# A four-layer graph network on one Trainium2 core: in the fourth layer, full-array work and weighted values for two steps at once, the log of the adjacency added by VectorE, norms issued behind the ReLUs

## The chip, the cores and the metric

The kernel runs on one core of one Trainium2 chip. A core has a matrix engine (TensorE, PE in the profile, with its weight loads listed as PEld), a vector engine (VectorE, DVE), a scalar engine (ScalarE, ACT), a general engine (GpSimd, POOL) and a queue engine (SyncE, SP) that issues transfers. Matmuls write into banks of PSUM, which the kernel uses as tiles of 128 partitions by 512 float32; everything else works from SBUF. All arithmetic here is float32. The metric is the time of one execution in device microseconds; before the change it is 2323.35 us, the median of three runs (2322.41, 2323.35, 2325.75).

## The reference: what is computed

`x` has 128 graphs of 64 nodes with 256 features. Four pre-norm layers run one after the other, `x = x + layer(relu(layernorm(x)))`. The first three (a graph convolution with batch norms, a spectral one, an LSTM over skips) are not touched but for one helper stage. The fourth is graph attention over 512 edges (`src`, `dst`), 4 heads of 64 features:

```python
Xq = (H @ W_lin.T).reshape(bt, n, h, dh)
Xv = (H @ W_val.T).reshape(bt, n, h, dh)
e = einsum('behd,hd->beh', leaky_relu(Xq[:, src] + Xq[:, dst], 0.2), a)
e = e + log(A0[src, dst] + 1e-8)          # A0 is the adjacency
attn = softmax of e over the edges that share a src
Y = segment_sum(attn * Xv[:, dst], src)   # per graph and head
return Y @ W_out.T
```

## The kernel before

All rows are 128 × 64 = 8192, held in SBUF as 16 blocks `X[i]` of 512 rows (128 partitions × 4 × 256). Layer 3 (`layer3`, line 2439) runs 32 steps `g`; each is half a block, four graphs. Eight steps form a group `q` (32 graphs, 4 heads: 128 partitions), whose edge scores lie in one PSUM bank, `acc`. Five banks `ps` go round for everything else, and one pool of weighted values (`y2`) has the rest.

What one step does, by its functions:

- `turned` (line 2494): layer norm of a block, `h`, on ScalarE with factors `n_r`, `n_m` from VectorE; eight transposes on TensorE, `ps<-ident,h`; two copies into `hT`, by `move`, which gives every other copy to VectorE and the rest to ScalarE; then a few sums `hS`.
- `queries` (line 2524): seven products (Strassen's scheme) that give queries `Q` and values `XV` of a block. The last three products come in `rest`, and after them `linear` (line 2558): a product `lin_p` and two reductions on VectorE.
- `score` (line 2573), called S here: for each of eight (64-row) operands a matmul with the edge matrix, `ps<-ed_S,Q`, and a ReLU on ScalarE, `r<-ps`. Two neighbours use the upper and lower half of the array's rows and run at the same time. The matmuls are 64 rows × 128 columns.
- `reduce` (line 2586): eight matmuls `acc<-r,ed_apad` (128 rows × 64 columns) weigh the ReLUs with `a` into `acc`. For the first step of a group a matmul with one row, `acc<-ed_log,ones`, starts the bank with the log of the adjacency.
- ten steps later (`LAG = 10`, `v = g - 10`) the attention of step `v`: `spread` makes four products `aw` on VectorE, `gathered` adds them up by eight matmuls `ps<-aw,ed_ODT` (128 × 64) and a copy `an` on ScalarE; `weighted` (line 2721), called W here, makes `y<-an,XV`, 16 small matmuls 64 × 64; `output` (line 2737) multiplies with `W_out` (`ps<-w_o,y`), adds to `X` on VectorE and stores to memory.
- behind the last step of a group `summed` adds the linear part, `softmax` (line 2654) runs two scans, an exponential, two more scans, a reciprocal and a product on VectorE; `edgewise` transposes the result.
- in the first eight steps `back` (line 2281) still brings in the third layer's result: two copies into `ls_t` (one buffer), eight transposes and two adds to `X`.

The loop calls these step by step. At even `g` TensorE gets S, W, reduce, gather, then the transposes of the next block and one output; at odd `g`, S, W, reduce, gather, then queries, one output and the rest of the queries. `turn` (line 2599) runs the last steps, with the last softmax done by another way, in an order written out by hand (`nc.ordered`).

The order of the instructions on each engine is set when the kernel is built: a scheduler of the tile framework places them by its own model, unless `hold` or `ordered` adds a fixed order between two instructions of an engine. In the trace each engine's instructions follow that order. Pools with `bufs=n` give a new tile the storage of the one n before, and its first writer waits for the last reader of that one. A helper at line 799 records all operations, so every group in the profile has that line and is told by its tiles.

Of the kernel before, what the change touches and what calls it, by code (L numbers as in the profile page):

```python
# [1465 lines left out]
class Kernel:  # L1466
# [924 lines left out]
    def edges(self, w, pool, psum):  # L2391
# [33 lines left out]
        self.mm(p[0:1, :], self.ones[:N, 0:1], ga)  # L2425
        self.logA = w.tile([1, E], F32, name="ed_log")
        eps = pool.tile([1, 1], F32, name="ed_eps")
        nc.vector.memset(eps[:], 1e-8)
        self.act(self.logA[:], p[0:1, :], AF.Ln, bias=eps[:])
# [9 lines left out]
    def layer3(self):  # L2439
        nc, o, io = self.nc, self.o, self.io  # L2440
        cx, (w,) = self.stage([("l3x", 1)], "tile")
        with cx:
            cy, pools = self.stage([("l3", 2), ("l3v", 2), ("l3s", 1), ("l3r", 6), ("l3ps", 5), ("l3cps", 1), ("l3yps", 1)], "tile")
            with cy:
# [15 lines left out]
                self.queries(st, 0, WQV, *pools)()  # L2460
                for g in range(8 * NG):
                    v = g - LAG
                    ahead = (g + 1) // 2 if g % 2 and g + 1 < 8 * NG else None
                    self.score(st, g, *pools)
                    if v >= 1:
                        self.weighted(st, v - 1, *pools)
                    self.reduce(st, g, *pools)
                    if g % 8 == 1 and 1 < g:
                        self.edgewise(st, g // 8 - 1, *pools)
                    if v >= 0:  # L2470
                        self.between(st, v, *pools)
                    if g % 8 == 7 and g + 1 < 8 * NG:
                        self.summed(st, g // 8, *pools)
                    if g < 8:
                        self.back(8 + g, pools[4], "ps")
                    if ahead:
                        rest = self.queries(st, ahead, WQV, *pools)
                    elif g + 2 < 8 * NG:
                        self.turned(st, g // 2 + 1, *pools)
                    if g + 6 == 8 * NG:  # L2480

                        p = pools[4].tile([P, BT], F32, name="ps")
                        for c in range(4):
                            self.nc.tensor.transpose(p[:N, c * P:(c + 1) * P], self.OST[:, c, :], self.ident[:])
                        self.act_copy(self.cont[:N, :], p[:N, :])
                    if v >= 1 and g + 1 < 8 * NG:
                        self.output(st, v - 1, WO, *pools)
                    if ahead:
                        rest()
                    if g % 8 == 7 and g + 1 < 8 * NG:  # L2490
                        self.softmax(st, g // 8, *pools)
                self.turn(st, WO, pools)

    def turned(self, st, i, pool, vp, sp, rp, psum, psc, psy):

        h = self.norm(pool, i)
# [76 lines left out]
    def score(self, st, g, pool, vp, sp, rp, psum, psc, psy):  # L2573

        rs = st["r"] = []
        Q = st["Q", g // 2]
        for fc in range(2):
            for k in range(4):
                s = slice(64 * (k % 2), 64 * (k % 2) + 64)
                p = psum.tile([P, E], F32, name="ps")  # L2580
                self.mm(p[:], Q[s, 2 * (g % 2) + k // 2, fc * P:(fc + 1) * P], self.S2[s, :])
                r = rp.tile([P, E], F32, name="r", bufs=8)
                self.act(r[:], p[:], AF.Relu)
                rs.append(r)

    def reduce(self, st, g, pool, vp, sp, rp, psum, psc, psy):
# [3 lines left out]
        if i == 0:  # L2590
            st["acc", q] = psc.tile([P, E], F32, name="acc")
            self.mm(st["acc", q][:], self.ones[0:1, :], self.logA[:], True, False)
        for fc in range(2):
            for k in range(4):
                z = 64 - 32 * (k // 2) - 4 * i
                x = 64 * (k % 2)
                self.mm(st["acc", q][x:x + 64, :], self.apad[:, fc, z:z + 64], st["r"][4 * fc + k][:], False, False)

    def turn(self, st, WO, pools):
# [8 lines left out]
        self.output(st, v - 2, WO, *pools)  # L2608
# [6 lines left out]
        self.weighted(st, v - 1, *pools)  # L2615
# [21 lines left out]
        self.weighted(st, v, *pools)  # L2637

        late = lambda: None
        for v in range(8 * NG - 8, 8 * NG + 2):  # L2640
# [7 lines left out]
            if v <= 8 * NG:  # L2648
                self.weighted(st, v - 1, *pools)
# [20 lines left out]
    def shifted(self, st, q, pool, vp, sp, rp, psum, psc, psy):  # L2670
# [4 lines left out]
        scan(m[:], self.drop[:], acc[:], -FLOOR, op0=ALU.add, op1=ALU.max)  # L2675
        scan(m2[:, ::-1], self.dropr[:, ::-1], acc[:, ::-1], -FLOOR, op0=ALU.add, op1=ALU.max)
        o.tt(m[:], m[:], m2[:], ALU.max)
        o.sub(e[:], acc[:], m[:])
# [42 lines left out]
    def weighted(self, st, g, pool, vp, sp, rp, psum, psc, psy):  # L2721

        a, V = st["a", g], st["V", g // 2]

        yp = psy.tile([P, 2, E], F32, name="y2")
        for m in range(2):
            for h in range(HEADS):
                for x in range(2):
                    s, z = slice(64 * x, 64 * x + 64), slice(64 * (h % 2), 64 * (h % 2) + 64)
                    f = (2 * m + h // 2) * N  # L2730
                    self.mm(yp[z, x, f:f + N], V[s, 2 * (g % 2) + m, h * N:(h + 1) * N], a[s, m, h, :])
        y = st["y", g] = vp.tile([P, 2, 2, 2, N], F32, name="y", bufs=3)
        for x in range(2):
            (self.move if g < 8 * NG - 11 else self.act_copy)(y[:, :, :, x, :].rearrange("p f m s -> p m f s"),
                      yp[:, x, 0:4 * N].rearrange("p (m f s) -> p m f s", m=2, f=2))

    def output(self, st, g, WO, pool, vp, sp, rp, psum, psc, psy, late=False):

        y = st["y", g]
        out = self.io["out"].rearrange("b n d -> (b n) d")  # L2740
        parts = []
        for lo, hi in ((0, 1), (1, 2)) if g == 8 * NG - 1 else ((0, 2),):
            p = psum.tile([P, 2, D], F32, name="ps")[:, 0:hi - lo, :]
            for m in range(lo, hi):
                for f in range(2):
                    self.mm(p[:, m - lo, :], y[:, f, m].rearrange("p x s -> p (x s)"), WO[:, f, :], f == 0, f == 1)
# [68 lines left out]
```

## Time and profile before

| what | value |
|---|---|
| three runs | 2322.41, 2323.35, 2325.75 us |
| the profiled execution | 2319.09 us, span 2317.3 us, granted TensorE clock 0.998 |
| TensorE busy in the span | 2275.7 us (98%) |
| VectorE, ScalarE busy | 1622.4 us (70%), 1145.9 us (49%) |
| layer 3 in the profile | 1735.6 us to the end |
| its steps without attention | 1747.5 to 1848.6 us (TensorE busy 100.8) |
| its loop with attention | 1874.2 to 2243.0 us (TensorE busy 368.1, VectorE 245.5, ScalarE 147.2) |
| its tail, `turn` | 2243.0 to 2317.3 us |

The page's first part gives busy time and share of the span for each engine. The chain of work goes back from the last instruction, at each step to what released it. A timeline gives start, duration, engine, line, operation, output<-inputs, shapes and count of a group of neighbouring instructions, and in brackets the idle time before them and what ended it. A float32 matmul has two records, so a count of 16 is eight matmuls.

### The profile page before, as it was taken

Reading aid. Unit: us, or ns where it says so; the run is one execution under the profiler, and the core shown is the slowest. Engines: PE = TensorE matmul, PEld = TensorE weight load, DVE = VectorE, ACT = ScalarE, POOL = GpSimd, SP = SyncE. Lnnn points to the kernel's source line nnn. Section 1 sums busy time; section 2 is a strip of 40 time slices with the busy share of each in tenths; the row PEclk is TensorE's granted clock in tenths of the full one; section 3 lists DMA queues with packets and bytes.
Section 4 is the critical chain, followed back from the end, with each engine's and each line's share of the span. In section 5 each row is a group of like instructions: output and inputs, shape, how many; then the busy total and the mean of one; then the engine's idle time right before and its main releaser. Section 6 shows DMA issues by size and latency. Waiting matters only on the chain.

```text
span 2317.3 us, 32619 instructions
## 1 busy us (share of the span) xinstructions
PE 2275.7 (98%) x12113; PEld 1626.8 (70%) x12113; DVE 1622.4 (70%) x4040; ACT 1145.9 (49%) x2501; POOL 7.1 (0%) x33
## 2 busy tenths in 40 slices
PE   7999997999999999999999999999999999999999
PEld 4554445677777788888999998888885544554554
DVE  8887676887457777766767667559756676767667
ACT  5667765754445654443444444336435544444321
POOL 1000000000000000000000000000000000000000
PEclk9999999999999999999999999999999999999999
DMA  5000220230000000001000002000010000000001
GB/s 176 1 1 28 64 55 25 71 83 28 1 28 1 1 19 1 1 1 37 1 1 1 1 1 73 1 1 17 1 52 22 1 5 15 15 19 14 15 23 46
DMA packets 61066, 54.81 MB, mean 24 GB/s; under 512 B 15203, under 2 KB 58724, under 8 KB 60900
## 3 DMA queue, kind: packets, MB, share of 16 engines
q1 hardware_dynamic: 60900, 52.66, 7.4%
q8 instruction: 97, 1.59, 0.3%
q14 instruction: 69, 0.57, 0.1%
HBM read 35.86 MB, written 16.78 MB: 23 GB/s over the span
## 4 chain that ended last, share of the span: by engine, by line
PE 79%; DVE 3%; ACT 1%; issue 1%; ACTq 0%; DVEq 0%
PE ps L799 69%; PE acc L799 5%; PE pt L799 4%; PE y L799 1%; PE pe L799 1%; DVE aw L799 1%; DVE X L799 1%; DVE sm_m L799 0%; DVE XV L799 0%; ACT ls_g L799 0%; ACT h L799 0%; DVE ls_g L799 0%; ACT big L799 0%; DVE sm_e L799 0%; DVE lin L799 0%
## 5 line engine op out<-in xcount | busy, mean ns | idle before, releaser
L799 ACT ACTIVATE ls_g<-ls_g,ls_b 128x512 f32<-128x512 f32 (+4 forms) x472 | 243.1, 565 | 150.7 <-DVE ls_g L799 148.9
L799 ACT ACTIVATE ls_g<-ps,ls_b 128x256 f32<-128x256 f32 (+3 forms) x268 | 115.3, 470 | 329.5 <-PE ps L799 326.3
L799 PE MATMUL ps<-z,w 128*128 128x512 f32 x512 | 254.2, 618 | 0.0
L799 PE MATMUL ps<-big,X 128*128 128x176 f32 (+3 forms) x848 | 212.9, 367 | 0.1
L799 DVE TENSOR_TENSOR ls_g<-ls_z,ps 128x512 f32<-128x512 f32 (+5 forms) x256 | 147.0, 579 | 91.9 <-PE ps L799 90.3
L799 PE MATMUL ps<-ls_tx,X 128*128 128x160 f32 (+2 forms) x960 | 207.1, 327 | 1.4 <-DVE ls_tx L799 0.9
L799 DVE TENSOR_TENSOR aw<-at,ed_OST 128x1024 f32<-128x1024 f32 x128 | 150.0, 1219 | 83.0 <-PE ps L799 82.8
L799 PE MATMUL ps<-X,X 128*128 128x160 f32 (+1 forms) x896 | 199.1, 306 | 0.0
L799 PE MATMUL ps<-X,ls_w 128*128 128x256 f32 x640 | 190.5, 379 | 0.0
L799 PEld LDWEIGHTS ps<-ls_tx,X 128*128 128x128 f32 x960 | 161.8, 190 | 16.2 <-DVE X L799 4.7
L799 PEld LDWEIGHTS ps<-big,X 128*128 128x128 f32 x848 | 146.1, 190 | 29.6 <-issue 19.3
L799 DVE TENSOR_TENSOR X<-ls_g 128x1024 f32<-128x1024 f32 (+2 forms) x108 | 117.4, 1087 | 49.8 <-ACT ls_g L799 49.8
L799 ACT ACTIVATE r<-ps 128x512 f32<-128x512 f32 x256 | 131.6, 616 | 41.5 <-PE ps L799 41.5
L799 PEld LDWEIGHTS ps<-X,X 128*128 128x128 f32 x896 | 148.6, 190 | 0.0
L799 PE MATMUL ps<-X,ls_s 128*128 128x256 f32 x480 | 142.3, 379 | 0.0
L799 PE MATMUL ps<-ls_tx,ls_s 128*128 128x256 f32 x464 | 134.9, 379 | 0.0
L799 PE MATMUL ps<-ed_S,Q 64*128 64x512 f32 x512 | 132.9, 618 | 1.4 <-DVE hT L799 0.7
L799 PE MATMUL ps<-ls_tx,ls_w 128*128 128x256 f32 x464 | 133.4, 380 | 0.0
L799 PEld LDWEIGHTS ps<-X,ls_w 128*128 128x128 f32 x640 | 121.7, 190 | 16.5 <-DVE X L799 0.3
L799 PEld LDWEIGHTS ps<-z,w 128*128 128x128 f32 x512 | 86.7, 189 | 66.2 <-issue 58.6
L799 PE MATMUL ps<-big,ls_w 128*128 128x256 f32 x464 | 132.0, 380 | 0.7 <-ACT ls_z L799 0.7
L799 PE MATMUL ps<-aw,ed_ODT 128*64 128x512 f32 x512 | 117.3, 595 | 0.1
(550 smaller groups left out, 4012.1 us busy)
## 6 DMA issues: line engine op xcount, KB each, us to landing
X<-in_x_dram SPq DMA_DIRECT2D x32, 512.0 KB
xs<-X SPq DMA_DIRECT2D x16, 512.0 KB
X<-xs SPq DMA_DIRECT2D x16, 512.0 KB
out_dram<-X SPq DMA_DIRECT2D x31, 256.0 KB
X<-in_L_gnn_Wih_t_dram SPq DMA_DIRECT2D x4, 512.0 KB
ls_w<-in_L_gnn_Wih_t_dram SPq DMA_DIRECT2D x4, 512.0 KB
ls_w<-in_L_gnn_Whh_t_dram SPq DMA_DIRECT2D x4, 512.0 KB
w<-in_L_gnn_W_t_dram SPq DMA_DIRECT2D x2, 512.0 KB
```

Source lines behind the costliest of these rows:

```text
L799: i = method(*a, **kw)
```

## The change

- **Log of the adjacency.** It is kept on 128 partitions in place of one, and VectorE adds it to `acc` in `shifted`; the matmul that started the bank goes, and the first two matmuls of a group start it.
- **Two steps at once.** W of steps `v-2` and `v-1` are issued together at even `g`, into one `y` tile of two steps (two buffers in place of three of one step). All full-array work of a pair of steps is issued at the end of the odd one: queries, the output of step `v-3`, the rest of the queries, transposes of the next block, the output of step `v-2`. The first two blocks are transposed ahead of the loop. Two `back`s are issued at each odd `g` below 8 in place of one at every `g`. The softmax's transposes come in the odd step behind the first output; those of `ed_OST` at step 27 in place of 26.
- **Tail.** `turn` issues three outputs where it issued one, since the loop leaves two more to it.
- **Norms.** `normed`, new, makes the norm of block `g // 2 + 2` at even `g` with its ScalarE instructions held behind the ReLUs that `score` has just issued.
- **Scores.** Of each pair the operand in the lower rows (`x = 1`) is multiplied first; the ReLUs keep their order.

```diff
--- before.py
+++ after.py
@@ -2422,11 +2422,11 @@
         ga = cmp[:N, :]
         o.mul(ga, p[:N, :], self.OD[:N, :])
         p = psum.tile([P, E], F32, name="pe")
-        self.mm(p[0:1, :], self.ones[:N, 0:1], ga)
-        self.logA = w.tile([1, E], F32, name="ed_log")
-        eps = pool.tile([1, 1], F32, name="ed_eps")
+        self.mm(p[:], self.ones[:N, :], ga)
+        self.logA = w.tile([P, E], F32, name="ed_log")
+        eps = pool.tile([P, 1], F32, name="ed_eps")
         nc.vector.memset(eps[:], 1e-8)
-        self.act(self.logA[:], p[0:1, :], AF.Ln, bias=eps[:])
+        self.act(self.logA[:], p[:], AF.Ln, bias=eps[:])
 
         ac = self.columns(pool, "ed_ac", io["L3_gnn_a"].rearrange("h d -> (h d)"))
         self.apad = w.tile([P, 2, P], F32, name="ed_apad")
@@ -2458,42 +2458,49 @@
                 self.turned(st, 0, *pools)
                 WQV = self.sums3(w, WQV)
                 self.queries(st, 0, WQV, *pools)()
+                self.turned(st, 1, *pools)
                 for g in range(8 * NG):
-                    v = g - LAG
-                    ahead = (g + 1) // 2 if g % 2 and g + 1 < 8 * NG else None
+                    v, odd, last = g - LAG, g % 2, g + 1 == 8 * NG
                     self.score(st, g, *pools)
-                    if v >= 1:
-                        self.weighted(st, v - 1, *pools)
+                    if not odd and g + 4 < 8 * NG:
+                        self.normed(st, g // 2 + 2, pools[0])
+                    if last:
+                        self.weighted(st, [v - 1], *pools)
+                    elif v >= 2 and not odd:
+                        self.weighted(st, [v - 2, v - 1], *pools)
                     self.reduce(st, g, *pools)
-                    if g % 8 == 1 and 1 < g:
-                        self.edgewise(st, g // 8 - 1, *pools)
                     if v >= 0:
                         self.between(st, v, *pools)
-                    if g % 8 == 7 and g + 1 < 8 * NG:
+                    if not odd or last:
+                        continue
+                    if g % 8 == 7:
                         self.summed(st, g // 8, *pools)
                     if g < 8:
-                        self.back(8 + g, pools[4], "ps")
-                    if ahead:
-                        rest = self.queries(st, ahead, WQV, *pools)
-                    elif g + 2 < 8 * NG:
-                        self.turned(st, g // 2 + 1, *pools)
-                    if g + 6 == 8 * NG:
+                        for i in (7 + g, 8 + g):
+                            self.back(i, pools[4], "ps")
+                    rest = self.queries(st, (g + 1) // 2, WQV, *pools)
+                    if g == 8 * NG - 5:
 
                         p = pools[4].tile([P, BT], F32, name="ps")
                         for c in range(4):
                             self.nc.tensor.transpose(p[:N, c * P:(c + 1) * P], self.OST[:, c, :], self.ident[:])
                         self.act_copy(self.cont[:N, :], p[:N, :])
-                    if v >= 1 and g + 1 < 8 * NG:
-                        self.output(st, v - 1, WO, *pools)
-                    if ahead:
-                        rest()
-                    if g % 8 == 7 and g + 1 < 8 * NG:
+                    if v >= 3:
+                        self.output(st, v - 3, WO, *pools)
+                    if g % 8 == 1 and 1 < g:
+                        self.edgewise(st, g // 8 - 1, *pools)
+                    rest()
+                    if g + 3 < 8 * NG:
+                        self.turned(st, (g + 3) // 2, *pools)
+                    if v >= 2:
+                        self.output(st, v - 2, WO, *pools)
+                    if g % 8 == 7:
                         self.softmax(st, g // 8, *pools)
                 self.turn(st, WO, pools)
 
     def turned(self, st, i, pool, vp, sp, rp, psum, psc, psy):
 
-        h = self.norm(pool, i)
+        h = st.pop("h", None) or self.norm(pool, i)
         hT = st["hT"] = pool.tile([P, 2, BT], F32, name="hT", bufs=1)
         for dc in range(2):
             p = psum.tile([P, BT], F32, name="ps")
@@ -2575,13 +2582,21 @@
         rs = st["r"] = []
         Q = st["Q", g // 2]
         for fc in range(2):
-            for k in range(4):
-                s = slice(64 * (k % 2), 64 * (k % 2) + 64)
-                p = psum.tile([P, E], F32, name="ps")
-                self.mm(p[:], Q[s, 2 * (g % 2) + k // 2, fc * P:(fc + 1) * P], self.S2[s, :])
-                r = rp.tile([P, E], F32, name="r", bufs=8)
-                self.act(r[:], p[:], AF.Relu)
-                rs.append(r)
+            for k in (0, 2):
+                ps = [psum.tile([P, E], F32, name="ps") for x in range(2)]
+                for x in (1, 0):
+                    s = slice(64 * x, 64 * x + 64)
+                    self.mm(ps[x][:], Q[s, 2 * (g % 2) + k // 2, fc * P:(fc + 1) * P], self.S2[s, :])
+                for x in range(2):
+                    r = rp.tile([P, E], F32, name="r", bufs=8)
+                    self.act(r[:], ps[x][:], AF.Relu)
+                    rs.append(r)
+
+    def normed(self, st, i, pool):
+
+        self.nc.hold((None, None, self.nc.mark()[2]))
+        st["h"] = self.norm(pool, i)
+        self.nc.hold()
 
     def reduce(self, st, g, pool, vp, sp, rp, psum, psc, psy):
 
@@ -2589,12 +2604,12 @@
         q, i = g // 8, g % 8
         if i == 0:
             st["acc", q] = psc.tile([P, E], F32, name="acc")
-            self.mm(st["acc", q][:], self.ones[0:1, :], self.logA[:], True, False)
         for fc in range(2):
             for k in range(4):
                 z = 64 - 32 * (k // 2) - 4 * i
                 x = 64 * (k % 2)
-                self.mm(st["acc", q][x:x + 64, :], self.apad[:, fc, z:z + 64], st["r"][4 * fc + k][:], False, False)
+                self.mm(st["acc", q][x:x + 64, :], self.apad[:, fc, z:z + 64], st["r"][4 * fc + k][:],
+                        i == 0 and fc == 0 and k < 2, False)
 
     def turn(self, st, WO, pools):
 
@@ -2605,14 +2620,15 @@
         W = [self.spread(st, v, c, *pools) for c in (0, 2)]
         self.summed(st, q, *pools)
         e, m, m2 = self.shifted(st, q, *pools)
-        self.output(st, v - 2, WO, *pools)
+        for u in (v - 4, v - 3, v - 2):
+            self.output(st, u, WO, *pools)
         self.gathered(st, v, W, *pools)
         et = m2[:].rearrange("p (c b) -> p c b", c=4)
         p = psum.tile([P, 4, P], F32, name="ps")
         for c in range(4):
             nc.tensor.transpose(p[:, c, :], e[:, c * P:(c + 1) * P], self.ident[:])
         self.act_copy(et, p[:])
-        self.weighted(st, v - 1, *pools)
+        self.weighted(st, [v - 1], *pools)
         W = [self.spread(st, v + 1, 0, *pools)]
         p = psum.tile([P, P], F32, name="ps")
         for c in range(4):
...
@@ -2672,10 +2688,11 @@
         nc, o, acc = self.nc, self.o, st["acc", q]
         e, m, m2 = (vp.tile([P, E], F32, name="sm_" + x, bufs=1) for x in ("e", "m", "m2"))
         scan = nc.vector.tensor_tensor_scan
-        scan(m[:], self.drop[:], acc[:], -FLOOR, op0=ALU.add, op1=ALU.max)
-        scan(m2[:, ::-1], self.dropr[:, ::-1], acc[:, ::-1], -FLOOR, op0=ALU.add, op1=ALU.max)
+        o.add(e[:], acc[:], self.logA[:])
+        scan(m[:], self.drop[:], e[:], -FLOOR, op0=ALU.add, op1=ALU.max)
+        scan(m2[:, ::-1], self.dropr[:, ::-1], e[:, ::-1], -FLOOR, op0=ALU.add, op1=ALU.max)
         o.tt(m[:], m[:], m2[:], ALU.max)
-        o.sub(e[:], acc[:], m[:])
+        o.sub(e[:], e[:], m[:])
         self.act(e[:], e[:], AF.Exp)
         return e, m, m2
 
@@ -2718,32 +2735,32 @@
         a = st["a", g] = vp.tile([P, 2, HEADS, N], F32, name="an")
         self.act(a[:], A[:], AF.Copy)
 
-    def weighted(self, st, g, pool, vp, sp, rp, psum, psc, psy):
-
-        a, V = st["a", g], st["V", g // 2]
-
-        yp = psy.tile([P, 2, E], F32, name="y2")
-        for m in range(2):
-            for h in range(HEADS):
-                for x in range(2):
-                    s, z = slice(64 * x, 64 * x + 64), slice(64 * (h % 2), 64 * (h % 2) + 64)
-                    f = (2 * m + h // 2) * N
-                    self.mm(yp[z, x, f:f + N], V[s, 2 * (g % 2) + m, h * N:(h + 1) * N], a[s, m, h, :])
-        y = st["y", g] = vp.tile([P, 2, 2, 2, N], F32, name="y", bufs=3)
+    def weighted(self, st, gs, pool, vp, sp, rp, psum, psc, psy):
+
+        yp = psy.tile([P, 2, 2, 4, N], F32, name="y2")
+        y = vp.tile([P, 2, 4, 2, N], F32, name="y", bufs=2)
+        for k, g in enumerate(gs):
+            a, V = st["a", g], st["V", g // 2]
+            st["y", g] = y, 2 * k
+            for m in range(2):
+                for h in range(HEADS):
+                    for x in range(2):
+                        s, z = slice(64 * x, 64 * x + 64), slice(64 * (h % 2), 64 * (h % 2) + 64)
+                        self.mm(yp[z, x, h // 2, 2 * k + m, :], V[s, 2 * (g % 2) + m, h * N:(h + 1) * N], a[s, m, h, :])
+        n = 2 * len(gs)
         for x in range(2):
-            (self.move if g < 8 * NG - 11 else self.act_copy)(y[:, :, :, x, :].rearrange("p f m s -> p m f s"),
-                      yp[:, x, 0:4 * N].rearrange("p (m f s) -> p m f s", m=2, f=2))
+            (self.move if gs[-1] < 8 * NG - 11 else self.act_copy)(y[:, :, 0:n, x, :], yp[:, x, :, 0:n, :])
 
     def output(self, st, g, WO, pool, vp, sp, rp, psum, psc, psy, late=False):
 
-        y = st["y", g]
+        y, k = st["y", g]
         out = self.io["out"].rearrange("b n d -> (b n) d")
         parts = []
         for lo, hi in ((0, 1), (1, 2)) if g == 8 * NG - 1 else ((0, 2),):
             p = psum.tile([P, 2, D], F32, name="ps")[:, 0:hi - lo, :]
             for m in range(lo, hi):
                 for f in range(2):
-                    self.mm(p[:, m - lo, :], y[:, f, m].rearrange("p x s -> p (x s)"), WO[:, f, :], f == 0, f == 1)
+                    self.mm(p[:, m - lo, :], y[:, f, k + m].rearrange("p x s -> p (x s)"), WO[:, f, :], f == 0, f == 1)
             parts.append((p, lo, hi))
 
         def add():
```

More of the change, by code (lines that the diff above doesn't have):

```diff
@@ L2636, in turn @@
         W = [self.spread(st, v + 2, 0, *pools)]
-        self.weighted(st, v, *pools)
+        self.weighted(st, [v], *pools)
         late = lambda: None
@@ L2648, in turn @@
             if v <= 8 * NG:
-                self.weighted(st, v - 1, *pools)
+                self.weighted(st, [v - 1], *pools)
             late = self.output(st, v - 2, WO, *pools, late=True)
```

## The prediction

> **What bounds the kernel now.** First the page: busy shares, then the chain that ended last.
>
> ```profile
> PE 2275.7 (98%) x12113; PEld 1626.8 (70%) x12113; DVE 1622.4 (70%) x4040; ACT 1145.9 (49%) x2501; POOL 7.1 (0%) x33
> ...
> PE 79%; DVE 3%; ACT 1%; issue 1%; ACTq 0%; DVEq 0%
> ```
>
> TensorE (PE) is busy throughout. An edit pays if it takes time out of PE's own sequence, and costs if it makes PE wait. Then the windows of layer 3 (start of the layer, steps without attention, first attention step, the loop, the tail; columns PE, PEld, VectorE, ScalarE, POOL, granted clock, DMA share, GB/s):
>
> ```profile
> 1747.50:1848.60 101.10, 100.80 (x469) 54.24 (x468) 64.69 (x140) 56.68 (x107) 0.00 (x0) 1.00 0.00 1
> 1848.60:1874.20 25.60, 24.86 (x106) 12.13 (x105) 22.05 (x40) 13.52 (x26) 0.00 (x0) 1.00 0.00 0
> 1874.20:2243.00 368.80, 368.11 (x2271) 189.08 (x2270) 245.47 (x349) 147.21 (x290) 0.00 (x0) 1.00 0.05 15
> 2243.00:2317.30 74.30, 70.69 (x632) 37.50 (x630) 57.28 (x61) 14.71 (x35) 0.00 (x0) 1.00 0.13 43
> ```
>
> In the loop PE idles 0.7 us in 368.8, VectorE is two thirds busy, the clock is full and DMA near zero. So I price PE stretch by stretch, by starts of its instruction groups. An odd step, in PE's timeline:
>
> ```profile
> 2034.16 3.60 PE L799 MATMUL ps<-aw,ed_ODT 128*64 128x512 f32 x16
> 2037.69 1.13 PE L799 MATMUL ps<-w_qv,hT 128*128 128x256 f32 x4
> ...
> 2044.70 1.03 PE L799 MATMUL ps<-w_qv,hS 128*128 128x256 f32 x4
> 2045.66 3.91 PE L799 MATMUL ps<-ed_S,Q 64*128 64x512 f32 x16
> 2049.50 0.69 PE L799 MATMUL y<-an,XV 64*64 64x64 f32 x32
> ```
>
> From 2037.69 (T below) the queries with one output take 7.97 us, the next scores (S) 3.84, the weighted values (W) 0.62. VectorE beside it:
>
> ```profile
> 2045.69 1.23 DVE L799 TENSOR_TENSOR lin_p<-Q,ed_a 128x1024 f32<-128x1024 f32 x1
> 2046.84 0.68 DVE L799 TENSOR_TENSOR XV<-XV,ps 128x512 f32<-128x512 f32 x1
> 2047.43 2.43 DVE L799 TENSOR_REDUCE lin<-lin_p 64x16 f32<-64x1024 f32 x2
> ```
>
> These end at 2049.86, T+12.17, 4.2 us after the queries have left PE. Nobody on PE waits for the reductions now. Last, two spots where PE waits for VectorE or an engine is late:
>
> ```profile
> 1856.08 3.35 DVE L799 RECIPROCAL sm_m<-sm_m 128x512 f32<-128x512 f32 x1
> ```
> ```profile
> 1858.09 1.98 PE L799 MATMUL ps<-ed_S,Q 64*128 64x512 f32 x6
> 1860.81 2.84 PE L799 MATMUL ps<-ed_S,Q 64*128 64x512 f32 x10 [0.74 <-DVE hT L799]
> ```
> ```profile
> 1766.02 1.28 DVE L799 TENSOR_TENSOR X<-X,ps 128x512 f32<-128x512 f32 x2 [3.27 <-PE ps L799]
> 1767.22 0.64 DVE L799 COPY ls_t<-big 128x512 f32<-128x512 f32 x1
> ```
>
> The scores at 1860.81 stood until VectorE, held by the softmax's reciprocal, had copied hT out of a `ps` bank: five banks rotate, and a late copy holds scores that have nothing to do with it.
>
> **What the change saves on PE.**
>
> - Log of the adjacency: the `acc<-ed_log,ones` pair took 1.05 us from start to next start, four times; one lay in a start wait. 3 × 1.05 = 3.2. VectorE's add instead is one 0.68 us row per softmax, hidden, but for the tail (below).
> - Array shapes: PE pays when the matmul's shape changes. Steady passes of S are 0.423 us apart, the first after a change 0.527, the last before one 0.52; so a change costs 0.14 to 0.20 (to S 0.20, S to W 0.14, W to reduce 0.16, gather to full array 0.20, to transposes 0.16). A pair of steps had eight, 1.36 us; now W of both steps and the full-array work come once, six, 1.05. 10 pairs × 0.31 = 3.1, and 0.15 in each of five early pairs, 0.8. S and W that were split around other work (at 1975.7 and 2114.0, 0.66 each; at 1873.1, 0.95) and softmax transposes between narrow matmuls (2 × 0.3) are gone too: 2.9. Sum 6.8.
> - Norms behind the ReLUs: in steps 1, 3, 5, 7 ScalarE alternates `h` (0.49 a piece) with the ReLUs and S takes 4.89 in place of 3.84; in step 9 5.49, in step 11 4.87. 4 × 1.05 + 1.6 + 1.0 = 6.8.
> - Turned pairs: in S of 2026.15 a weight load waited 0.71 for a ReLU; with the bank that comes free later asked for first, both matmuls of a pair run side by side. Bounds for S: 0.527 + 6 × 0.423 + 0.52 = 3.58 and today's 3.84 to 3.90; I take 3.65, as ReLUs at 0.48 each still pace it, for the eleven odd steps that no other term touches: 11 × 0.22 = 2.4.
>
> Saved: 19.2 us. [...] Eight ReLUs at 0.48 take 3.9 us on ScalarE alone, more than S itself. [...]
>
> **What it costs.**
>
> - *Scores of even steps behind VectorE.* The odd step now runs queries, output, rest, transposes of the next block, output, and then S of the even step. The second half of hT is copied by VectorE, whose built order has it behind `lin_p` and both reductions. S would start at T + 7.97 + 0.87 (transposes) + 1.73 (output) = T+10.57, its second pair of matmuls at T+11.53, into the bank that the hT copy frees: T + 12.17 + 0.68 + 0.05 = T+12.9. The third pair needs the output's bank, added by VectorE next, at T+13.5. S becomes 5.1 in place of 3.84. Steps 14, 20, 22, 28: +1.22 each = 4.9. Steps 0, 2, 4, 6 (no outputs, but the same order; fourth pair late, S about 5.2): +1.35 each = 5.4. Behind the softmaxes (16, 24) two scans of 1.2 come ahead of the output's add: +2.0 each = 4.0. Steps 18 and 26 +0.75, 8 −0.15, 10 +0.55, 12 +1.05, 30 +0.25 by the same sum with their own fillings. Together 17.5. Ends: 0 if VectorE reaches the copy before T+11.5; 25 if each pair of every step also waits for its own add.
> - *Two `back`s in one step.* `ls_t` is one buffer. The second eight transposes need its refilling: by 1765.32 → 1767.86 VectorE ends it 2.54 after the first group's start, as two X adds (1.28) stand before it. Without the wait they would come after 0.93. With 0.1 to be released: +1.7, 4 times, 6.9. Ends: 3.2 (copy ahead of the adds, 1.75) and 8.3 (ScalarE's copy of 1.1 last).
> - *Norms ahead of the next ReLUs.* `normed` puts the square root and four `h` in ScalarE's order behind this step's ReLUs and so before the next step's. They wait for VectorE's factors. At step 9 the factors stand behind the softmax's 3.35 reciprocal: `h` would be done 27.3 after the full-array start of step 7, the first ReLU is due at 19.8: up to 7.5; lower end 3.35; I take 5.5, as VectorE's statistics may run earlier. Step 1 +0.8 (1.28 table load), step 11 +1.1, steps 17 and 25 +1.6 each (scans ahead). Together 10.6. Ends 0 and 14.
> - *Tail.* Two outputs move from the loop (−3.46) into `turn`, where VectorE is continuous from 2244 to 2250: three adds for one and the log add delay the softmax's later pieces by 3.5 to 3.75: +0.15. Start and the softmax of step 7: +1.3. Wider log (128 rows rather than 1): earlier stage, off the chain, 0.
>
> [...] At 1860.08 the hT copy ran only after the reciprocal and its product, and PE idled 0.74. [...]
>
> **Sum.** Costs 17.5 + 6.9 + 10.6 + 1.5 = 36.5, saved 19.2: +17.3. All durations are from the profiled execution (span 2317.3, 1.8 around it, 2319.1 in all), which lies 4.3 below the median of 2323.35; 2336.4 by its clock, 2340.6 against the median. I say 2340.
>
> DMA: `out` stores of two outputs a step go at once rather than one by one; SP's queue carries little (DMA share 0.05) and only the last store ends the span, where the tail is as before. POOL has nothing in the loop. Cost 0; without that cover a 256 KB store's landing would count, once.
>
> **Rivals.**
>
> 1. *The hT copy holds nobody* (other side). VectorE reaches the copy by T+11.5, or PE's order puts other work there. Then 17.5 goes: 2323, and with turned pairs at 3.65 in even steps perhaps 3 less, 2320: not slower. It decides where the copy ends: below 4.7 in all, a mean of 0.3 a step (copy done by T+11.9), the kernel is not slower by what can be told. For: the row at 1860.81 shows only 0.74 for a delay of 3.35. Against: T+12.17 for the reductions is measured, and the copy is behind them.
> 2. *VectorE becomes the bound.* The gathers wait for products `aw` (1.14 each). In a common pair the statistics end at about T+21.2 and the first product is released by T+22.1: 0.9 slack. If the waits push VectorE past it, each of ten pairs pays about 1: 2350. For: slack of 0.9 beside a 1.2 shift. Against: VectorE is idle 123 of 369 us in the loop, and PE's own waits give the slack back.
> 3. *No blocking by norms.* VectorE runs the factors early enough at steps 9, 17, 25: 10.6 goes: 2330. For: today's factors in common steps follow within 1 us of their inputs. Against: at 1862.37 they came after the reciprocal.
>
> That the change does not do what it says can hardly be: the removed matmuls have rows of their own.
>
> **How the numbers follow.** Mine 0.52 (range 2331 to 2350: ends of the three costs, taken half together); rival 1 0.22; rival 2 0.13; rival 3 0.13. A measurement here can tell 0.2%, 4.65 us, from no change. Faster (below 2318.7) takes half of rival 1 and a little of the ends, 0.13; same, the rest of rival 1 and part of rival 3, 0.15; slower 0.72. The range reaches from rival 1's lower part, 2319, to rival 2's middle, 2350, leaving out some 0.08 and 0.10.
>
> **What would show it.** Right: S of even steps 4.9 to 5.3 from start to next start with a weight load waiting for VectorE's hT; odd S 3.6 to 3.7; W as one group of 64 per pair; 2.5 between two `ls_t` groups; some 4 to 8 us of PE idle before S of step 9 with ScalarE on `h`; no `ed_log` rows on PE. Wrong: even S at or under 3.9 (rival 1); first gather passes waiting for `aw` (rival 2); S of step 9 as long as others (rival 3).

## The result and the profile after

The changed kernel takes 2347.52 us (median of five runs, 2345.04 to 2347.85) against 2323.35 us before: slower, ratio 1.0106, 95% interval 1.0095 to 1.0117. The forecast was 2340, from 2319 to 2350. The profiled execution took 2347.85 us, span 2346.1.

The first part of the page after, and the engines of its chain:

```profile
PE 2284.4 (97%) x12105; PEld 1633.6 (70%) x12105; DVE 1626.4 (69%) x4034; ACT 1148.1 (49%) x2490; POOL 7.2 (0%) x33
...
PE 75%; DVE 6%; ACT 1%; issue 1%; DMA 0%; DVEq 0%; ACTq 0%
```

VectorE's part of the chain doubled, from 3 to 6%, though its busy time is the same (1622.4 and 1626.4): it has become late at some places, not busier. The windows of the steps without attention, of the first attention steps and of the loop (columns as in the table before):

```profile
1753.90:1863.90 110.00, 100.91 (x467) 54.78 (x466) 65.27 (x139) 59.72 (x106) 0.00 (x0) 1.00 0.00 1
1863.90:1895.90 32.00, 26.87 (x108) 13.67 (x106) 19.95 (x38) 13.48 (x25) 0.00 (x0) 0.84 0.00 1
1895.90:2269.00 373.10, 366.55 (x2243) 188.91 (x2243) 253.73 (x383) 153.04 (x292) 0.00 (x0) 1.00 0.04 14
```

PE was idle for 0.3 us of the 101 before the softmaxes begin; now it is idle for 9.1 of 110. In the loop, 0.7 became 6.5.

**How the runs are compared.** Layer 3 starts between 1735.6 and 1742.6 us in the profiles below, though the layers ahead of it are the same but for one small matmul. So beside the times I give the length of layer 3: from its first transposes (`ps<-ident,h`, at 1735.62 before, at 1741.10 after) to the start of the last group of matmuls in PE's timeline, in one profile of each kernel. Before 574.5, after 597.7: 23.3 longer, near what the medians say (24.2).

Nearly all of that is in the scores, S: their start-to-next-start lengths add up to 132.0 us before and 154.9 after. The same sum over the even steps is 63.1 and 81.2, over the odd ones 68.9 and 73.7, where step 9 alone went from 5.49 to 11.68. The `ls_t` transposes went from 7.4 to 13.9, and the log's matmuls (4.2) are gone.

**An even S.** PE, its weight loads and VectorE around step 20 of the changed kernel, from their timelines:

```profile
2099.95 1.04 PE L799 MATMUL ps<-ident,h 128*128 128x128 f32 x8
2100.83 1.89 PE L799 MATMUL ps<-w_o,y 128*128 128x256 f32 x8
2102.65 1.98 PE L799 MATMUL ps<-ed_S,Q 64*128 64x512 f32 x6
2105.03 2.99 PE L799 MATMUL ps<-ed_S,Q 64*128 64x512 f32 x10 [0.40 <-DVE hT L799]
```
```profile
2105.03 0.30 PEld L799 LDWEIGHTS ps<-ed_S,Q 64*128 64x128 f32 x4 [1.23 <-DVE hT L799]
2105.75 0.44 PEld L799 LDWEIGHTS ps<-ed_S,Q 64*128 64x128 f32 x4 [0.42 <-DVE X L799]
2106.90 0.18 PEld L799 LDWEIGHTS ps<-ed_S,Q 64*128 64x128 f32 x1 [0.71 <-ACT r L799]
```
```profile
2101.82 2.43 DVE L799 TENSOR_REDUCE lin<-lin_p 64x16 f32<-64x1024 f32 x2
2104.29 0.69 DVE L799 COPY hT<-ps 128x512 f32<-128x512 f32 x1
2105.01 0.69 DVE L799 TENSOR_TENSOR X<-X,ps 128x512 f32<-128x512 f32 x1
```

The second matmul of the second pair stands until the hT copy ends at 2104.98, behind both reductions; the second of the third pair until the output's add at 2105.70; the last matmul then waits for a ReLU. S is 5.31. The weight loads of S in all, what they waited for, by the view of that tile (us, times), before and after:

```profile
  ACT r L799: 23.1, 45
  DVE XV L799: 3.0, 4
  DVE hT L799: 2.7, 3
...
  DVE X L799: 0.8, 3
```
```profile
  ACT r L799: 27.1, 56
  DVE hT L799: 21.8, 24
  DVE X L799: 9.3, 9
```

**Step 9.** VectorE, ScalarE and PE of the changed kernel from their timelines, and PE's windows (the last three figures are granted clock, DMA share and GB/s):

```profile
1872.04 3.35 DVE L799 RECIPROCAL sm_m<-sm_m 128x512 f32<-128x512 f32 x1
...
1876.64 0.16 DVE L799 SCALAR_TENSOR_TENSOR n_m<-n_mv,n_r 128x4 f32<-128x4 f32 x1
```
```profile
1876.83 2.07 ACT L799 ACTIVATE h<-X,n_m,n_r 128x256 f32<-128x256 f32 x4 [6.09 <-DVE n_m L799]
1878.81 2.02 ACT L799 ACTIVATE r<-ps 128x512 f32<-128x512 f32 x4
```
```profile
1871.47 2.84 PE L799 MATMUL ps<-ed_S,Q 64*128 64x512 f32 x10
1879.44 3.77 PE L799 MATMUL ps<-ed_S,Q 64*128 64x512 f32 x6 [5.13 <-ACT r L799]
1883.14 5.24 PE L799 MATMUL acc<-r,ed_apad 128*64 128x512 f32 x16
```
```profile
1874.30:1879.40 5.10, 0.01 (x1) 0.00 (x0) 4.25 (x16) 2.57 (x6) 0.00 (x0) 0.68 0.00 0
1879.40:1883.10 3.70, 3.66 (x6) 1.64 (x6) 0.00 (x0) 2.52 (x5) 0.00 (x0) 0.50 0.00 0
1883.10:1888.30 5.20, 5.20 (x17) 1.43 (x16) 0.00 (x0) 1.08 (x2) 0.00 (x0) 0.68 0.00 0
```

The norm's factors come behind the softmax's reciprocal, `h` behind them, the ReLUs behind `h`, and PE stands for 5.13 us. Its clock is then 0.50 through S and into the reduce, which takes 5.17 in place of 3.58.

**Two backs.** PE's timeline in an odd step below 8:

```profile
1771.26 1.09 PE L799 MATMUL ps<-ident,ls_t 128*128 128x128 f32 x8
1773.82 1.09 PE L799 MATMUL ps<-ident,ls_t 128*128 128x128 f32 x8 [1.46 <-DVE ls_t L799]
```

2.56 from one to the next, where 0.93 had been enough.

### The profile page after: what moved, and what is told of

Same layout as the page of the kernel before. It is cut to its first block, busy times and chain, and to the rows that moved or that the text cites. A ratio compares the mean times of both kernels' runs of the same rounds, so it can differ in the third digit from the quotient of the medians.

```text
span 2346.1 us, 32571 instructions
## 1 busy us (share of the span) xinstructions
PE 2284.4 (97%) x12105; PEld 1633.6 (70%) x12105; DVE 1626.4 (69%) x4034; ACT 1148.1 (49%) x2490; POOL 7.2 (0%) x33
## 4 chain that ended last, share of the span: by engine, by line
PE 75%; DVE 6%; ACT 1%; issue 1%; DMA 0%; DVEq 0%; ACTq 0%
PE ps L799 66%; PE acc L799 5%; PE pt L799 4%; DVE sm_m L799 1%; DVE lin L799 1%; DVE X L799 1%; PE pe L799 1%; PE y L799 1%; DVE lin_p L799 1%; DVE XV L799 1%; ACT h L799 0%; DVE aw L799 0%; DVE hT L799 0%; DVE Q L799 0%; ACT ls_g L799 0%
## 5 line engine op out<-in xcount | busy, mean ns | idle before, releaser
L799 PE MATMUL ps<-ed_S,Q 64*128 64x512 f32 x512 | 142.7, 629 | 14.5 <-DVE hT L799 5.9
L799 PEld LDWEIGHTS ps<-ed_S,Q 64*128 64x128 f32 x512 | 59.2, 187 | 87.9 <-issue 34.5
```

The costliest lines, as they stand in the source:

```text
L799: i = method(*a, **kw)
```

## The experiments

Twelve kernels, against the kernel before on the same chip. "Changed" is the kernel of the diff.

| kernel | median, us | ratio to before, 95% | layer 3, us |
|---|---|---|---|
| before | 2323.35 | | 574.5 |
| changed | 2347.52 | 1.0095 to 1.0117 | 597.7 |
| changed, linear part late | 2336.62 | 1.0043 to 1.0077 | 586.8 |
| changed, norms early | 2334.65 | 1.0036 to 1.0070 | 586.4 |
| changed, second back late | 2340.99 | 1.0064 to 1.0098 | 593.6 |
| changed, pairs not turned | 2339.32 | 1.0064 to 1.0097 | 591.7 |
| changed, one back a step | 2338.71 | 1.0057 to 1.0089 | 591.4 |
| changed, seven banks | 2324.25 | 0.9994 to 1.0012 | 574.8 |
| mended (four edits) | 2313.35 | 0.9948 to 0.9973 | 563.2 |
| mended, pairs turned | 2310.24 | 0.9938 to 0.9967 | 565.0 |
| mended, two ReLUs on VectorE | 2324.64 | 1.0002 to 1.0021 | 576.2 |
| mended, seven banks | 2301.53 | 0.9890 to 0.9923 | 552.5 |
| mended, seven banks, turned | 2302.69 | 0.9902 to 0.9933 | 552.6 |
| before, log on VectorE | 2324.05 | 1.0001 to 1.0019 | 577.1 |

My theory, A: even scores wait for VectorE's hT copy, norms hold the ReLUs behind a softmax, the second back waits for its buffer. The rivals are told with each run.

### The linear part behind the transposes

```diff
-            self.linear(st, i, pool, vp, sp, rp, psum, psc, psy)   # at the end of rest()
                     if v >= 2:
                         self.output(st, v - 2, WO, *pools)
+                    self.linear(st, (g + 1) // 2, *pools)
```

> The linear part (its product and two reductions on VectorE) is issued behind the next block's transposes and the second output, so that VectorE's order has the hT copy ahead of the reductions; nothing else moves. Theory A (even scores wait for the hT copy behind the reductions): in the changed kernel the sixteen even S hold 18.5 us above 3.92 each; with the copy ending at about T+10.5 rather than T+12.9 they come down to 3.9 to 4.2, and the time falls by 14 to 18 us, to about 2331. Rival (the even scores are slow for another cause, ScalarE's pace or the banks behind the output's add): S stays above 5 in steps 14, 20, 22, 28 and the time falls by less than 4. Second rival (the reductions only move the wait to the products aw): S is short, but the gathers wait, gain below 8.

Layer 3 is 11.0 us shorter. VectorE and PE in the steady loop of this kernel:

```profile
2060.05 0.68 DVE L799 COPY hT<-ps 128x512 f32<-128x512 f32 x1
2060.65 1.20 DVE L799 TENSOR_REDUCE lin<-lin_p 64x16 f32<-64x1024 f32 x1
```
```profile
2060.87 3.95 PE L799 MATMUL ps<-ed_S,Q 64*128 64x512 f32 x16
2064.76 1.16 PE L799 MATMUL y<-an,XV 64*64 64x64 f32 x64
```

S is in one piece, 3.88 in steps 14, 20, 22 and 28, 3.90 in steps 2, 4 and 6; the even steps' sum fell from 81.2 to 65.3, by 15.9. That is theory A's step, and the rival (another cause) is out. But 5.3 us came back in odd steps: S of step 17 went from 4.85 to 6.58, of step 25 from 4.84 to 8.03. The reductions now run later, with them the softmax, and its reciprocal and the norm behind it (ScalarE's `h` waits for the factors, and the ReLUs, from 2145.08, stand behind `h`):

```profile
2137.34 3.35 DVE L799 RECIPROCAL sm_m<-sm_m 128x512 f32<-128x512 f32 x1
```
```profile
2142.62 2.07 ACT L799 ACTIVATE h<-X,n_m,n_r 128x256 f32<-128x256 f32 x4 [0.68 <-DVE n_m L799]
```

Where the norms are made earlier as well (the mended kernels), both S are 3.90 to 3.92.

### The norms one step earlier

```diff
-                    if not odd and g + 4 < 8 * NG:
-                        self.normed(st, g // 2 + 2, pools[0])
+                    if (not odd and g % 8 or not g or g % 8 == 7) and g + 4 < 8 * NG:
+                        self.normed(st, (g + 1) // 2 + 2, pools[0])
```

> The norms that the changed kernel makes at steps 8, 16, 24, behind a softmax on VectorE, are made one step earlier, behind the ReLUs of steps 7, 15, 23 and ahead of the softmax. Theory A (norms waiting for factors behind the softmax hold the next ReLUs): S of step 9 falls from 11.68 to about 4, its reduce from 5.17 to 3.6, S of steps 17 and 25 from 4.85 to 3.92: 11 us less, about 2336. Rival (VectorE itself is late there with Q or hT, and the norms only share the wait): S of step 9 stays above 8 and the gain is under 4.

11.4 us shorter, as A had it. PE's timeline at step 9 of this kernel:

```profile
1871.48 3.98 PE L799 MATMUL ps<-ed_S,Q 64*128 64x512 f32 x16
1875.40 3.65 PE L799 MATMUL acc<-r,ed_apad 128*64 128x512 f32 x16
```

S of step 9 is 3.92, its reduce 3.58, S of steps 17 and 25 3.92.

### The two backs

```diff
                         if g < 8:
-                            for i in (7 + g, 8 + g):
-                                self.back(i, pools[4], "ps")
+                            self.back(7 + g, pools[4], "ps")
...
                     rest()
+                    if g < 8:
+                        self.back(8 + g, pools[4], "ps")
```

> The second back of steps 1, 3, 5, 7 is issued behind the rest of the queries in place of directly behind the first one. Theory A (its transposes wait for the one buffer ls_t to be filled again): the two groups of ls_t transposes of a step take 0.9 each and no longer 2.5 for the first, 6.5 us less in the four steps; some of it may come back as even S waiting longer for VectorE, which has two more adds ahead of the hT copy: total gain 3 to 6.5, about 2342. Rival (the banks, freed by adds to X, are what is late): the wait only moves, gain under 1.5.

The two groups of transposes take 7.2 us in all in place of 13.9, but layer 3 is only 4.1 shorter: the wait moved. In the changed kernel with this edit VectorE adds the second back ahead of its hT copy (VectorE, then PE):

```profile
1782.51 1.28 DVE L799 TENSOR_TENSOR X<-X,ps 128x512 f32<-128x512 f32 x2
1783.72 0.68 DVE L799 COPY hT<-ps 128x512 f32<-128x512 f32 x1
```

S of steps 2, 4, 6 and 8 went from 5.17, 5.17, 5.17 and 3.94 to 7.54, 7.49, 5.93 and 6.18: 7.7 longer in all, more than the 6.7 that the transposes won. Layer 3 is shorter all the same because of step 9, which the edit was not meant for. In ScalarE's new order three of its ReLUs stand ahead of `h`; its S is 3.92 in place of 11.68, and the wait for `h` comes in the reduce, which takes 8.57:

```profile
1876.98 1.93 PE L799 MATMUL acc<-r,ed_apad 128*64 128x512 f32 x6
1881.23 4.40 PE L799 MATMUL acc<-r,ed_apad 128*64 128x512 f32 x10 [2.31 <-ACT r L799]
```

That is 4.4 less for the two together. So I returned to one back a step, at the end of even steps too:

```diff
+                    if g < 8:
+                        self.back(8 + g, pools[4], "ps")
                     if not odd or last:
                         continue
-                    if g < 8:
-                        for i in (7 + g, 8 + g):
-                            self.back(i, pools[4], "ps")
```

> One back at every step below 8 as in the kernel before, ahead of the odd step's other full-array work; all else as changed. Theory A (two backs in a row wait for the one buffer ls_t): 64 ls_t transposes take 7 to 8 us in all and no longer 13.9, against one more change of the array's shape in even steps (0.15 each): 5 to 6 us less, about 2341. Rival (the work added ahead of the hT copy matters more than the buffer, as when the second back was put behind the queries): even S of steps 2 to 8 lengthen and the gain is under 2.

6.4 us shorter, S as in the changed kernel but for 0.3 more in steps 7 and 15. The buffer's wait was worth 6 us, and the work put ahead of the hT copy was dearer than the buffer in the first try.

### The pairs not turned

```diff
-                for x in (1, 0):
+                for x in (0, 1):
```

> The pairs of the scores are multiplied upper rows first, as in the kernel before; all else as changed. The prediction's own step (turned pairs make S 0.2 shorter): odd S goes from 3.92 to 4.1 or more, 2 to 4 us slower, 2350. Rival (ScalarE's ReLUs, eight at 0.48, pace S whichever half comes first): odd S stays 3.9 and the time within 1 us.

Neither: 6.1 us *shorter*. Odd S is 3.90 against 3.92, so turning brought nothing there; even S of steps 14, 20, 22 and 28 is 4.64 against 5.31. The even steps hold 3.4 of the 6.1; another 1.8 lies in step 9 (S 10.56 for 11.68, its reduce 4.53 for 5.17), where the clock was at 0.50 for 6.8 us and no longer 10.2, and 0.5 in step 1. The weight loads of such an S without turning:

```profile
2098.12 0.29 PEld L799 LDWEIGHTS ps<-ed_S,Q 64*128 64x128 f32 x2 [0.72 <-ACT r L799]
2098.64 0.29 PEld L799 LDWEIGHTS ps<-ed_S,Q 64*128 64x128 f32 x3 [0.22 <-DVE hT L799]
```

The trace does not name the banks, but the waits tell which engine each matmul waited for. In the turned S of step 20 above, the fourth waits for the hT copy and the sixth for the output's add. Here the fourth waits for the first ReLU, and the fifth for the hT copy. The late bank comes a place later: the fourth matmul starts 1.87 after S (at 2098.12), and the wait for hT holds the fifth until 2.39; turned, nothing but the third runs from 0.96 until the hT copy lets the fourth go at 2.38.

### All four edits

> All four undone or mended: linear part behind transposes and second output, norms of steps 8, 16, 24 one step earlier, one back a step, scores' pairs not turned; the log on VectorE, the weighted values of two steps and the full-array work of two steps stay. Theory A (the costs are these and the savings of the prediction are real: 3.2 log, 6.8 array shapes, 6.8 norms out of the ReLUs): even and odd S 3.9, time 2347.5 - 16 - 12 - 6 = about 2313, some 9 us under the kernel before. Rival (the savings are not real, the new order has its own price): 2322 or more.

2313.35 us, ratio 0.9960: faster than before. Layer 3 is 34.6 us shorter than changed; the four edits one by one gave 11.0, 11.4, 6.4 and 6.1, 34.8. That the two agree so closely is in part chance: the early norms also win back most of the 5.3 that the late linear part lost in odd steps, and beside these edits turning costs 1.8 and not 6.1 (next run). The costs lie in these four places, then, and what is left is a saving: 11.3 us under the kernel before. The prediction's savings without the turned pairs, less its 1.5 for tail and start, come to 15.3; S of step 0, for one, still takes 5.39 for 3.84. How much of the 11.3 is the log's was not tried by itself. A steady pair of steps takes 33.50 against 33.74 with S 0.06 longer: 0.30 for two changes of shape less, where the prediction had 0.31.

> As the one before, with the scores' pairs turned as in the changed kernel. Theory A after the first runs (turning costs because it asks first for the bank that VectorE frees late, and gains nothing as ScalarE paces S): with the hT copy early the two orders are within 1 us. The prediction's own step: turned is 2 to 5 us faster.

1.8 us longer in layer 3 than not turned (565.0 and 563.2), the times' intervals overlap. With the hT copy early the order of the pairs hardly matters.

### What paces S

S was 3.84 to 3.92 in every undisturbed step, not 3.65. Two of the ReLUs on VectorE:

```diff
-                    self.act(r[:], ps[x][:], AF.Relu)
+                    if 4 * fc + k + x in (3, 7):
+                        self.o.ts(r[:], ps[x][:], 0.0, ALU.max)
+                    else:
+                        self.act(r[:], ps[x][:], AF.Relu)
```

> As the mended kernel, with two of each step's eight ReLUs on VectorE (maximum with zero) in place of ScalarE. If ScalarE's 0.48 a ReLU paces S, odd S falls from 3.9 to about 3.6 where VectorE is free, up to 8 us in all, less what waits for VectorE in even steps. If the array paces S, odd S stays 3.9 and the time is the same or longer.

Odd S stayed 3.90, and layer 3 grew by 13.0 us, as the reduces (122.0 us in all against 112.5) and gathers (119.9 against 115.0) waited for VectorE. The test was badly chosen, though: when five banks go round, the third and fourth pair of S take the banks of ReLUs 0, 1 and 2, and I had moved 3 and 7. It doesn't tell ScalarE from the banks. This does:

```diff
-            ("l3ps", 5), ("l3cps", 1), ("l3yps", 1)
+            ("l3ps", 7), ("l3cps", 1)
...
-        yp = psy.tile([P, 2, 2, 4, N], F32, name="y2")
+        yp = [psum.tile([P, 2, 4, N], F32, name="ps") for x in range(2)]
```

> The mended kernel with the two PSUM banks that only the weighted values used put into the common pool: seven banks go round in place of five, and the weighted values take two of them per pair of steps. If S is paced by the way of the first ReLU back to the sixth matmul's bank (five banks), S falls from 3.9 to the unhindered 3.6 in nearly all 32 steps, 6 to 10 us less, about 2304. If the array or ScalarE's sum of eight ReLUs paces S, it stays at 3.9 and the time within 2 us. Beside it the transposes and outputs have more banks too: even S wait less for VectorE.

2301.53 us, ratio 0.9906, the best of all. PE's timeline in its loop:

```profile
2067.31 3.70 PE L799 MATMUL ps<-ed_S,Q 64*128 64x512 f32 x16
2070.95 1.16 PE L799 MATMUL ps<-an,XV 64*64 64x64 f32 x64
...
2079.06 3.70 PE L799 MATMUL ps<-ed_S,Q 64*128 64x512 f32 x16
```

S is 3.63 in thirty of 32 steps, even and odd, with the same eight ReLUs on ScalarE. So the wait for a bank that a ReLU gives back paced S: its weight loads waited 13.1 us for ReLUs in the mended kernel and 3.8 in this one. With pairs turned:

> Seven banks with the scores' pairs turned. If turning matters only where the second bank of a pair comes free later than the first, it makes no difference where no bank is waited for: within 1 us of the run before. If turning has a price or gain of its own in the array, S differs from it by 0.05 or more in every step, 2 us or more in all.

552.6 against 552.5, and S the same in 30 steps: with seven banks turning made no difference. Last, seven banks in the changed kernel alone:

> The changed kernel with one edit: the weighted values' two banks go into the common pool (seven banks in place of five); VectorE's order, the norms and the two backs stay as changed. If the even scores wait because a bank comes round too soon, not because of VectorE's order by itself, seven banks move the hT copy's bank from the second pair of S to the third: T+12.9 against 12.4, so even S falls from 5.3 to 4.1 to 4.3, odd S to 3.63, S of step 9 stays long (it waits for ReLUs behind the norms): 16 to 22 us less, about 2328. If the scores need the hT copy or VectorE in another way, even S stays above 5 and only the odd ones gain: 4 to 6 us.

2324.25 us: 23.0 us of layer 3 come back by one edit. Even S is 4.29 or 4.30 in steps 14, 20, 22 and 28, odd S 3.63 but for steps 1, 9, 11, 17 and 25, S of step 9 still 10.28:

```profile
1871.91 2.07 PE L799 MATMUL ps<-ed_S,Q 64*128 64x512 f32 x2 [4.58 <-ACT r L799]
```

So the even scores waited for banks that came round too soon, not for the hT copy itself, and step 9 is another thing, the order on ScalarE.

### The log alone

The four hunks on the log, put into the kernel before (log on 128 partitions, `o.add(e, acc, logA)` in `shifted`, no matmul at the group's start).

> The kernel before with one part of the change alone: the log of the adjacency on 128 partitions, added by VectorE in the softmax in place of the matmul that starts the bank. The prediction's own step: three of the four matmul pairs, 1.05 us each, lie on the path, VectorE's add is hidden but for the last softmax (0.7): 2.5 to 3.2 us less. Rival (the add delays a softmax that something waits for, at steps 9 and 17 and in the tail): no gain, within 1 us.

The rival: layer 3 is 2.6 us *longer*, ratio 1.0010 (1.0001 to 1.0019). The matmuls (4.2) are gone, but S grew by 5.1: steps 8, 16 and 24 by 0.8, 1.5 and 0.7, steps 9, 17 and 25 by 0.5, 0.4 and 1.2, and the tail loses half a microsecond. PE's and VectorE's timelines at step 9, where PE before had waited 0.74:

```profile
1862.18 2.84 PE L799 MATMUL ps<-ed_S,Q 64*128 64x512 f32 x10 [1.24 <-DVE hT L799]
```
```profile
1857.45 3.35 DVE L799 RECIPROCAL sm_m<-sm_m 128x512 f32<-128x512 f32 x1
1860.83 0.69 DVE L799 TENSOR_TENSOR sm_e<-sm_e,sm_m 128x512 f32<-128x512 f32 x1
1861.44 0.68 DVE L799 COPY hT<-ps 128x512 f32<-128x512 f32 x1
```

The matmul's time goes on PE, but the softmax, and the hT copy behind it, end later where VectorE was already late for PE. Only the sum was tried: whether the add alone or the scheduler's new order after it (step 8's S is split around other work there) has the larger part is open.

## Why the prediction was right, and where it was not

- **Even scores (17.5):** right. The copy was forecast to end at T+12.86 and the add at T+13.5; with T = 2092.08 (S's start less 10.57) that is 2104.94 and 2105.58, measured 2104.98 and 2105.70. S is 5.31 where I had 5.1 (I left out the fourth pair's wait for a ReLU behind the third), 5.94 in steps 16 and 24 for 5.84. Moving the reductions took 15.9 out of the even steps. Rival 1 is out. That the size fits so well is in part luck: the even steps lost 18.1 (63.1 to 81.2) with the pairs turned and would have lost 14.7 without (77.8), and my sum did not reckon with their order.
- **Two backs (6.9):** right, 6.5 in the rows and 6.4 by undoing it.
- **Norms ahead of the next ReLUs (10.6):** right in place, and in size by luck. The early norms free steps 9, 17 and 25, for which I had 5.5, 1.6 and 1.6, together 8.7; undoing gave 11.4. For step 9 I took a loss of 5.5; PE idled 5.13. What the term left out is the clock: S and most of the reduce ran on at 0.50, and the step lost 7.8 in S and 1.6 in the reduce, 9.3 by comparison with the kernel whose norms are early. Steps 17 and 25 lost 0.9 each. Rival 3 is out. No ReLU of step 9 passed the waiting `h`: PE began S at 1871.47, ScalarE ran `h` from 1876.83 and the ReLUs from 1878.81.
- **Turned pairs (a saving of 2.4):** wrong in sign. It brought nothing in odd steps and cost 6.1 by undoing it, 3.4 of that in even S. I had priced the order where banks are free early, and not in the even steps, where it gives the banks that VectorE frees late to earlier matmuls: the very steps of the first cost. A second engine was not tested on the ReLUs that matter; two more banks, with all ReLUs on ScalarE, brought S to 3.63, close to the 3.58 I had as the unhindered end.
- **Log (a saving of 3.2):** the rows are gone, but "hidden but for the tail" is wrong: alone it costs 2.6, as the softmax, and behind it hT, come later. What it does beside the rest of the change no run shows.
- **Array shapes (6.8):** right in size where it can be read, 0.30 a steady pair for 0.31 (3.1 of the 6.8); the rest of the term was not read by itself.
- **Norms out of the ReLUs (6.8):** S of steps 3, 5 and 7 came down from 4.90 to 3.92, of step 11 from 4.87 to 4.39; step 1 stayed at 4.83, as its table load (1.28 at 1760.51, 0.8 in the costs) ate the gain; step 9 is told above.
- **Sum:** 17.3 forecast, 24.2 measured (23.3 in layer 3). The 6 us between 17.3 and 23.3 are two things by the rows. In step 9 I had 3.9 (5.5 less the 1.6 of norms moved out), and 7.6 came: 6.2 in S, 1.4 in the reduce. And the 2.4 of the turned pairs did not come in the odd steps. What else was off nearly cancels.
- **Rival 2** (gathers wait for `aw`) did not come: the gathers take 115.1 us in all before and 115.0 after.

## What to carry to other kernels

When work of two steps is put together on the full engine, look at what the helpers hand back behind it: here a matmul waited for a bank that another engine emptied late, because that engine's queue had long, unhurried reductions (2.43 us) ahead of a short copy (0.69). Move the unhurried work behind the copy, and look for banks that a seldom used tile keeps to itself; two of them in the common pool were worth 23.0 us in the changed kernel, more than any one reordering (11.4 at most), and still 10.7 after all four. An instruction issued early is only free if its inputs are early too: in step 9 `h` waited 6.09 us for its factors, the ReLUs stood behind it, and PE was idle for 5.13.

## What the runs showed of the hardware that I had not expected

A single wait of 5.13 us in an otherwise full stretch was followed by a halved clock of TensorE: granted 0.50 from 1876.14 to 1886.38, and 1.00 again from there (0.68 in the last window of step 9 is the mean of both). Passes of the reduce were 0.85 to 0.91 us apart at first and 0.43 at the end; the reduce took 5.17 in place of 3.58. The halving began when PE had stood for only 1.83 us, and shorter waits had it too. In the kernel with the linear part late, a wait of 2.09 us in step 25 was followed by 3.41 us at 0.50 (0.63 in the mean of 2145.00 to 2149.60), and S is 8.03; S of step 17, with a wait of the same length, is 6.58. In the kernel with the second back late, 3.41 us at 0.50 (from 1783.49) followed a wait of 0.69, ahead of which PE had issued two matmuls in 2.6 us; the six matmuls behind that wait took 5.02. The four waits of 1.46 for `ls_t` in the changed kernel had none (granted 1.00 from 1753.90 to 1863.90). So the length of a wait did not tell by itself whether the clock would be halved, and a pause in PE's work cost more than its length: 9.3 us in step 9 for the 5.13.

With five banks S was held by banks, not by its matmuls: 3.84 to 3.92 in undisturbed steps, against 3.63 with seven in all but two steps of the mended kernel, whichever half of a pair goes first.
